# Attention products in 32-wide groups, and experts without a software pipeline

## The chip, the cores and the metric

The kernel runs on one core of a Trainium2 chip. Its time is device time in microseconds, from start to end of one execution. The core's engines run side by side, each with its own queue in strict order: TensorE (PE in the profile) multiplies matrices, with its weight loads shown apart as PEld; VectorE (DVE), ScalarE (ACT) and GpSimd (POOL) do elementwise work; SyncE (SP) issues the DMAs. Engines wait for each other by semaphores. TensorE multiplies a stationary operand of up to 128 rows (the contraction) by 128 columns (the outputs) with a moving operand and writes to PSUM, which has eight banks of 512 fp32 values in each of 128 partitions. All data here is fp32.

## The reference: a convolutional attention block, then attention and experts

The input is eight images of 256 channels by 32 x 32 pixels (1024 positions). Layer 0 normalizes each image, makes queries, keys (4 heads of 32) and values (4 heads of 64) by a 1x1 convolution, attends over all 1024 positions, adds a depthwise 3x3 convolution of the values, projects, and adds the result to the image:

```python
attn = jnp.einsum('bhkn,bhkm->bhnm', q, k) * SCALE
attn = jax.nn.softmax(attn, axis=-1)
out = jnp.einsum('bhdm,bhnm->bhdn', v, attn).reshape(B, Cc, H, W)
```

Then comes an FFN: a 1x1 convolution to 1024 channels, a depthwise 3x3 convolution, GELU of one half times the other, a 1x1 convolution back, and a filter in the Fourier domain of 8 x 8 patches. Layer 1 is causal attention over 1024 positions with 256 channels, followed by eight experts. Each expert is a chain of three matrices with a normalization and a ReLU after the first two; a weight per expert and position (`w`) mixes the outputs:

```python
h = jnp.einsum('bfd,edh->bfeh', x, W1) + b1
h = jax.nn.relu(_bn(h, g1, be1, m1, v1))
h = jnp.einsum('bfeh,ehk->bfek', h, W2) + b2
h = jax.nn.relu(_bn(h, g2, be2, m2, v2))
y = jnp.einsum('bfeh,ehd->bfed', h, Wo) + bo
return jnp.einsum('bfed,fe->bfd', y, w)
```

## The kernel before

The 256 channels lie in two groups of 128 partitions; positions run along the free dimension. `fast_body` does the work in three stages.

**Layer 0** goes image by image. `attend(b, c, fill)` (L381) takes half an image's queries, 512 of them, at a time. For each pair of heads `g` and each of eight key tiles `m` it makes a step: two logit products (L393), one per head, with the head's 32 rows of `qk` as the contraction, so that each sits on its own 32 rows of the array; one exponential on ScalarE for both (L395); and two value products (L397) that contract over the 128 keys. The stationary operand of the latter has 128 columns: 64 of values and 64 of ones, from a buffer `vT` that holds values, ones, values side by side. So one product gives a head's output and, in the other 64 rows, the sums for the softmax. There are 32 steps an image. The logits `s` have two buffers of two PSUM banks, the accumulators two banks, and all other products share two banks (`ps_m`, tag "mm"). After the eight key tiles ScalarE copies outputs and sums out (L404 to L407). `finish` (L409) divides by the sums: two reductions, a reciprocal, a product with `selh` that spreads the reciprocals over the channels (L418), then the projection.

After each step `attend` calls `fill` (L513). It draws pieces from generators that hold other work: `ffn` of the image before (`before`), `prologue` of the image after (`after`: norm, queries, keys, values, transposes of the values and the depthwise convolution), and `finish` of the half before (`late`). The share drawn grows with the number of the step, over STEPS = 32. A scheduler then orders instructions for each engine when the program is built, with these positions as priorities; at run time each engine works its list in order. The FFN's two depthwise convolutions a group are nine VectorE operations each (L462 and L464), from padded images `hpad` that ScalarE fills (L452). GELU (L472), the square root of the norms (L315) and the exponential make ScalarE change its function table, shown as ACT_TABLE_LOAD.

**Layer 1's attention** (L597) isn't touched by the change.

**The experts** (L754) run 128 units: 8 experts x 8 images x 2 halves of 512 positions. A unit has three layers of four products each (two output groups by two contraction groups): layer 1 (`pm<-z,w1s`), layer 2 (`pm<-h,w2s`), both at L724 with a ReLU on ScalarE (L728), and the output product (`pye`, L745), followed by a VectorE operation (L749) and an addition on GpSimd (L750). `advance(n)` (L731) is a software pipeline written by hand: it issues layer 1 of unit n, then layer 2 of unit n-1, then the output product of unit n-2. So between a layer and the next one of the same unit there are eight products of other units. All of them draw on one pool of eight PSUM banks.

Of the kernel before, what the change touches and what calls it, by code (L numbers as in the profile page):

```python
# [15 lines left out]
P = 128  # L16
# [62 lines left out]
def fast_body(  # L79
# [95 lines left out]
    with ExitStack() as l0:  # L175
# [3 lines left out]
        ps_s = l0.enter_context(tc.tile_pool(name="ps_s0", bufs=2, space=PSUM))  # L179
# [78 lines left out]
        def one_hot(dst, mult):  # L258
            nc.gpsimd.affine_select(
                out=dst,  # L260
                in_=dst,
                compare_op=ALU.not_equal,
                fill=1.0,
                base=0,
                pattern=[[-mult, dst.shape[1]], [0, dst.shape[2]]],
                channel_multiplier=1,
            )
# [3 lines left out]
        selh = rows_to("selh", 4, HD)  # L271
        one_hot(selh, 32)
# [9 lines left out]

        vts = []
        for i in range(2):
            v_ = one.tile([P, NT, KC, 3, HD], F32, tag=f"vT{i}", name=f"vT{i}")
            nc.gpsimd.memset(v_[:, :, :, 1, :], 1.0)
            vts.append(v_)

# [49 lines left out]
        def prologue(b):  # L338
# [5 lines left out]
            vT = vts[b % 2]  # L344
# [14 lines left out]
            for g in range(KC):  # L359
                for j0 in range(0, NT, 4):  # L360
                    tp = ps_m.tile([P, 4, 2, HD], F32, tag="mm", name="tpv")
                    for j in range(4):
                        nc.tensor.transpose(
                            tp[:, j].rearrange("p s d -> p (s d)"), o[:, g, (j0 + j) * P : (j0 + j + 1) * P], ident
                        )
                    nc.scalar.copy(vT[:, j0 : j0 + 4, g, 0:3:2, :], tp)
                yield
# [13 lines left out]
        def attend(b, c, fill):  # L381

            qk, vT, o = st[b]
            cs = slice(c * HALF, (c + 1) * HALF)
            sm = two.tile([P, HALF], F32, tag="sm", name="sm")
            ou = None
            for g in range(KC):
                acc = [ps_a.tile([P, HALF], F32, tag=f"acc{i}", name=f"acc{i}") for i in range(2)]
                for m in range(NT):
                    s = ps_s.tile([P, 2, HALF], F32, tag="s", name="s")  # L390
                    for i in range(2):
                        kp = slice((2 * g + i) * KD, (2 * g + i + 1) * KD)
                        nc.tensor.matmul(s[:, i, :], qk[kp, 1, m * P : (m + 1) * P], qk[kp, 0, cs], start=True, stop=True)  # L393
                    p = two.tile([P, 2, HALF], F32, tag="p", name="p", bufs=3)
                    nc.scalar.activation(p, s, AF.Exp)  # L395
                    for i in range(2):
                        nc.tensor.matmul(  # L397
                            acc[i], vT[:, m, g, i : i + 2, :], p[:, i, :], start=(m == 0), stop=(m == NT - 1)
                        )
                    fill()  # L400
                if g == 0:
                    ou = two.tile([P, KC, HALF], F32, tag="ou", name="ou", bufs=1)

                nc.scalar.copy(sm[64 * g : 64 * g + 32, :], acc[0][64:96, :])  # L404
                nc.scalar.copy(ou[0:64, g, :], acc[0][0:64, :])
                nc.scalar.copy(sm[64 * g + 32 : 64 * g + 64, :], acc[1][0:32, :])
                nc.scalar.copy(ou[64:128, g, :], acc[1][64:128, :])  # L407

            def finish():  # L409
# [6 lines left out]
                for g in range(KC):  # L416
                    bc = ps_m.tile([P, HALF], F32, tag="mm", name="bc")
                    nc.tensor.matmul(  # L418
                        bc, selh[:, 2 * g : 2 * g + 2, :], sm, start=True, stop=True
                    )  # L420
                    nc.vector.tensor_mul(ou[:, g, :], ou[:, g, :], bc)
                    nc.vector.tensor_add(o[:, g, cs], o[:, g, cs], ou[:, g, :])
                    nc.scalar.activation(t[:, g, cs], t[:, g, cs], AF.Identity, bias=proj_o[:, g : g + 1])
# [85 lines left out]
        STEPS = CH * KC * NT  # L509
        for b in range(B):  # L510
            step = [0]

            def fill():  # L513
                step[0] += 1
                i = step[0]
                if late is not None:
                    late.step()
                if i > 3 and before is not None:
                    before.to((i - 3) / (STEPS - 4))
                if after is not None:  # L520
                    after.to((i - 4) / (STEPS - 6))

# [174 lines left out]
    with ExitStack() as l2:  # L697
# [17 lines left out]


        units, hidden = [], {}

        def layer(name, w_, src, sc, bi, e):
            dst = hp.tile([P, KC, HALF], F32, tag=name, name=name, bufs=3)  # L720
            for g in range(KC):
                pm = ps.tile([P, HALF], F32, tag="mm", name="pm")
                for k in range(KC):
                    nc.tensor.matmul(  # L724
                        pm, w_[:, k, g * P : (g + 1) * P], src[:, k, :], start=(k == 0), stop=(k == KC - 1)
                    )
                c = KC * e + g
                nc.scalar.activation(dst[:, g, :], pm, AF.Relu, bias=bi[:, c : c + 1], scale=sc[:, c : c + 1])  # L728
            return dst

        def advance(n):  # L731
            if n <= len(units):
                e, b, h, w1s, w2s, wos, wb = units[n - 1]
                hidden[n - 1] = layer("h1", w1s, z[b][:, :, h * HALF : (h + 1) * HALF], s1, o1, e)
            if 0 <= n - 2 < len(units):
                e, b, h, w1s, w2s, wos, wb = units[n - 2]
                hidden[n - 2] = layer("h2", w2s, hidden[n - 2], s2, o2, e)
            if 0 <= n - 3:
                e, b, h, w1s, w2s, wos, wb = units[n - 3]
                h2 = hidden.pop(n - 3)  # L740
                hs = slice(h * HALF, (h + 1) * HALF)
                for g in range(KC):
                    py = ps.tile([P, HALF], F32, tag="mm", name="pye")
                    for k in range(KC):
                        nc.tensor.matmul(  # L745
                            py, wos[:, k, g * P : (g + 1) * P], h2[:, k, :], start=(k == 0), stop=(k == KC - 1)
                        )
                    y = hp.tile([P, HALF], F32, tag="y", name="y", bufs=3)
                    nc.vector.scalar_tensor_tensor(y, py, col("bo", KC * e + g), wb[:, hs], ALU.add, ALU.mult)  # L749
                    nc.gpsimd.tensor_add(t[b][:, g, hs], t[b][:, g, hs], y)  # L750
                if e == NE - 1 and h == 1:
                    nc.sync.dma_start(ov[b], t[b])

        for e in range(NE):  # L754
# [13 lines left out]
            for b in range(B):  # L768
                for h in range(2):
                    units.append((e, b, h, w1s, w2s, wos, wb))  # L770
                    advance(len(units))
        for i in range(2):
            advance(len(units) + 1 + i)
# [690 lines left out]
```

## Time and profile before

| | us |
|---|---|
| median of 3 runs | 3958.95 (3957.77 to 3959.01) |
| the profiled execution's own time | 3958.95 |
| its span in the trace | 3957.2 |
| TensorE busy | 3600.7 |
| VectorE busy | 1734.9 |
| ScalarE busy | 1349.2 |
| exponentials of layer 0 (L395), 256 of 1.022 | 255.0 |
| value and sum products (L397), 1024 records | 507.6 |
| logit products (L393), 1024 records | 316.2 |

A group line of the profile reads: line, engine, operation, output<-inputs, size of output<-input, count; then busy time in us and mean ns of one; then the engine's idle time before the group and what ended it. A matmul's size stands as rows*columns of the stationary operand, then the moving operand. Every fp32 product leaves two matmul records and two weight-load records. Records of TensorE overlap: the start of the next tells what one costs, and its length includes the drain. "PEclk" is the granted share of TensorE's clock.

### The profile page before, as it was taken

How to read it: one execution, taken by the hardware profiler on the slowest of the kernel's cores; microseconds unless marked ns; L12 is line 12 of the kernel's file. 1: busy time of each engine (PE TensorE's matmuls, PEld its weight loads, DVE VectorE, ACT ScalarE, POOL GpSimd, SP SyncE). 2: the span in 40 equal slices, each digit the busy share in tenths (PEclk: the TensorE clock that was granted, in tenths of full speed). 3: DMA queues.
4: the chain of work that ended last, by engine and by line, in shares of the span. 5: the costliest groups of instructions: out<-in, count | busy, mean ns of one | idle time of the engine just before them, and what ended most of it. 6: DMA issues, size and time to landing. Idle time of an engine off the chain costs nothing.

```text
span 3957.2 us, 25092 instructions
## 1 busy us (share of the span) xinstructions
PE 3600.7 (91%) x9780; PEld 1652.5 (42%) x9780; DVE 1734.9 (44%) x1946; ACT 1349.2 (34%) x1754; POOL 512.1 (13%) x483
## 2 busy tenths in 40 slices
PE   7999999999999998388878888889999999999998
PEld 4334343434343434244444444444444444444443
DVE  3377777676767685634444444321111111111111
ACT  4354545454545452021111112222333333333332
POOL 1000000000000000011112211122222222222222
PEclk9999999999999998688898889979999999999999
DMA  1000000000000000020000000000000000000001
GB/s 60 0 0 22 0 22 0 22 0 22 0 22 0 11 0 11 12 92 0 0 0 0 0 0 0 0 16 3 6 8 0 8 3 6 8 0 8 0 26 60
DMA packets 16277, 45.04 MB, mean 11 GB/s; under 512 B 1350, under 2 KB 9494, under 8 KB 14102
## 3 DMA queue, kind: packets, MB, share of 16 engines
q1 hardware_dynamic: 16150, 43.36, 3.0%
q8 instruction: 79, 1.29, 0.1%
q14 instruction: 48, 0.39, 0.0%
HBM read 26.57 MB, written 16.78 MB: 11 GB/s over the span
## 4 chain that ended last, share of the span: by engine, by line
PE 71%; DVE 19%; ACT 4%; issue 2%; POOL 2%; DMA 1%; ACTq 0%; SPq 0%; DVEq 0%; POOLq 0%
PE pm L724 22%; PE pye L745 11%; DVE conv L464 9%; PE acc L397 7%; PE s L393 3%; PE ph L330 3%; PE s L630 3%; PE po L661 3%; DVE o L377 3%; PE pq L607 3%; PE pz L480 3%; PE pq L330 2%; PE var L574 2%; DVE r L577 1%; PE pv L617 1%
## 5 line engine op out<-in xcount | busy, mean ns | idle before, releaser
L728 ACT ACTIVATE h<-pm,bn_o,bn_s 128x512 f32<-128x512 f32 x512 | 398.5, 778 | 894.1 <-PE pm L724 894.1
L749 DVE SCALAR_TENSOR_TENSOR y<-pye,vec,wb 128x512 f32<-128x512 f32 x256 | 192.1, 750 | 1148.0 <-PE pye L745 1148.0
L464 DVE SCALAR_TENSOR_TENSOR conv<-hpad,vec,conv 128x1024 f32<-128x1024 f32 x512 | 648.5, 1279 | 9.4
L397 PE MATMUL acc<-p,vT 128*128 128x512 f32 x1024 | 507.6, 628 | 62.3 <-ACT p L395 61.9
L724 PE MATMUL pm<-z,w1s 128*128 128x512 f32 x1024 | 463.0, 595 | 0.0
L724 PE MATMUL pm<-h,w2s 128*128 128x512 f32 x1024 | 460.3, 592 | 0.0
L745 PE MATMUL pye<-h,wos 128*128 128x512 f32 x1024 | 460.2, 592 | 0.0
L750 POOL TENSOR_TENSOR t<-t,y 128x512 f32<-128x512 f32 x256 | 324.3, 1267 | 1031.3 <-DVE y L749 1031.3
L397 PEld LDWEIGHTS acc<-p,vT 128*128 128x128 f32 x1024 | 192.2, 197 | 338.8 <-issue 173.0
L395 ACT ACTIVATE p<-s 128x1024 f32<-128x1024 f32 x256 | 255.0, 1022 | 218.0 <-PE s L393 217.1
L393 PE MATMUL s<-qk 32*128 32x512 f32 x1024 | 316.2, 632 | 0.0
L724 PEld LDWEIGHTS pm<-z,w1s 128*128 128x128 f32 x1024 | 194.7, 191 | 249.1 <-issue 192.4
L724 PEld LDWEIGHTS pm<-h,w2s 128*128 128x128 f32 x1024 | 194.6, 190 | 244.9 <-issue 213.6
L745 PEld LDWEIGHTS pye<-h,wos 128*128 128x128 f32 x1024 | 194.6, 190 | 244.9 <-issue 244.9
L330 PE MATMUL ph<-xn,piw 128*128 128x512 f32 x512 | 246.1, 613 | 18.1 <-ACT hpad L452 18.1
L630 PE MATMUL s<-kk,q 128*128 128x512 f32 x512 | 236.4, 597 | 10.4 <-DVE pr L648 5.6
L574 PE MATMUL var<-sq,mean_c 128*128 128x512 f32 x128 | 107.6, 946 | 123.8 <-POOL sq L571 123.8
L558 POOL MEMSET ones<- 1x128 f32 x1 | 0.2, 194 | 1633.3 <-DVE conv L464 1633.3
L393 PEld LDWEIGHTS s<-qk 32*128 32x128 f32 x1024 | 93.0, 184 | 180.3 <-issue 165.5
L377 DVE SCALAR_TENSOR_TENSOR o<-vpad,pe_w,o 128x1024 f32<-128x1024 f32 x128 | 161.8, 1275 | 0.3
L330 PEld LDWEIGHTS ph<-xn,piw 128*128 128x128 f32 x512 | 95.4, 194 | 157.3 <-issue 127.4
L480 PE MATMUL pz<-pow__122,hid 128*128 128x256 f32 x512 | 121.9, 389 | 42.8 <-DVE hid L473 42.8
(177 smaller groups left out, 3239.0 us busy)
## 6 DMA issues: line engine op xcount, KB each, us to landing
t<-in_x_dram SPq DMA_DIRECT2D x8, 1024.0 KB, 4.9
sp<-t SPq DMA_DIRECT2D x8, 1024.0 KB, 3.9
t<-sp SPq DMA_DIRECT2D x8, 1024.0 KB, 9.9
out_dram<-t SPq DMA_DIRECT2D x8, 1024.0 KB, 4.0
w1s<-in_w_dram SPq DMA_DIRECT2D x8, 256.0 KB, 2.7
w2s<-in_w_dram SPq DMA_DIRECT2D x8, 256.0 KB, 2.8
wos<-in_wo_dram SPq DMA_DIRECT2D x8, 256.0 KB, 2.7
piw<-in_pi_wT_dram SPq DMA_DIRECT2D x1, 1024.0 KB, 8.7
```

Source lines behind the costliest of these rows:

```text
L330: nc.tensor.matmul(ps, w[:, k, o0 : o0 + P], src[:, k, hs], start=(k == 0), stop=(k == KC - 1))
L377: nc.vector.scalar_tensor_tensor(d3, src, wk, d3, ALU.mult, ALU.add)
L393: nc.tensor.matmul(s[:, i, :], qk[kp, 1, m * P : (m + 1) * P], qk[kp, 0, cs], start=True, stop=True)
L395: nc.scalar.activation(p, s, AF.Exp)
L397: nc.tensor.matmul(acc[i], vT[:, m, g, i : i + 2, :], p[:, i, :], start=(m == 0), stop=(m == NT - 1))
L464: nc.vector.scalar_tensor_tensor(d3, src, wk, d3, ALU.mult, ALU.add)
L480: nc.tensor.matmul(pz[:, k, :], hid[g][:, (2 * n + k) * P : (2 * n + k + 1) * P], pow_[:, g, :], start=(g == 0), stop=(g == ng - 1),)
L630: nc.tensor.matmul(s[:, hs], q[:, k, q0 : q0 + P], kk[:, k, hs], start=(k == 0), stop=(k == KC - 1))
L724: nc.tensor.matmul(pm, w_[:, k, g * P : (g + 1) * P], src[:, k, :], start=(k == 0), stop=(k == KC - 1))
L728: nc.scalar.activation(dst[:, g, :], pm, AF.Relu, bias=bi[:, c : c + 1], scale=sc[:, c : c + 1])
L745: nc.tensor.matmul(py, wos[:, k, g * P : (g + 1) * P], h2[:, k, :], start=(k == 0), stop=(k == KC - 1))
L750: nc.gpsimd.tensor_add(t[b][:, g, hs], t[b][:, g, hs], y)
```

## The change

Two edits. In layer 0 the attention steps are cut differently: a step now covers all four heads, two key tiles and 256 queries. There are four logit products per key tile, each on its own 32 rows of the array (L395 of the new kernel), and two exponentials of 128 x 1024. The values are taken in pieces of 32 channels, so that each product writes 32 output partitions on its own 32 columns of the array, with four pieces for each pair of heads (L406). The sums are products of their own, with a stationary operand of 32 columns, 16 of them ones (L413). The ones between the values are gone. There are 16 steps an image instead of 32, the logits have one buffer of four banks instead of two of two, the accumulators and sums take one bank each, and the shares in `fill` are set anew. In the experts, the pipeline is taken out: each unit does layer 1, layer 2 and the output product in turn (L754 and L769 of the new kernel).

```diff
-        ps_s = l0.enter_context(tc.tile_pool(name="ps_s0", bufs=2, space=PSUM))
+        ps_s = l0.enter_context(tc.tile_pool(name="ps_s0", bufs=1, space=PSUM))
...
+        ones32 = wpool.tile([P, 2, 32], F32, name="ones32")
+        nc.gpsimd.memset(ones32, 0.0)
+        for c in range(2):
+            nc.gpsimd.memset(ones32[:, c, 16 * c : 16 * c + 16], 1.0)
...
-            for g in range(KC):
-                acc = [ps_a.tile([P, HALF], F32, tag=f"acc{i}", name=f"acc{i}") for i in range(2)]
-                for m in range(NT):
-                    s = ps_s.tile([P, 2, HALF], F32, tag="s", name="s")
+            for part in range(2):
+                ps_ = slice(c * HALF + part * QC, c * HALF + (part + 1) * QC)
+                acc = ps_a.tile([P, KC, QC], F32, tag="acc", name="acc")
+                for m2 in range(NT // 2):
+                    s = ps_s.tile([P, NH, 2, QC], F32, tag="s", name="s")
                     for i in range(2):
-                        kp = slice((2 * g + i) * KD, (2 * g + i + 1) * KD)
-                        nc.tensor.matmul(s[:, i, :], qk[kp, 1, m * P : (m + 1) * P], qk[kp, 0, cs], start=True, stop=True)
-                    p = two.tile([P, 2, HALF], F32, tag="p", name="p", bufs=3)
-                    nc.scalar.activation(p, s, AF.Exp)
+                        m = 2 * m2 + i
+                        for hd in range(NH):
+                            kp = slice(hd * KD, (hd + 1) * KD)
+                            nc.tensor.matmul(
+                                s[:, hd, i, :], qk[kp, 1, m * P : (m + 1) * P], qk[kp, 0, ps_], start=True, stop=True
+                            )
+                    p = two.tile([P, NH, 2, QC], F32, tag="p", name="p")
+                    for g in range(KC):
+                        nc.scalar.activation(p[:, 2 * g : 2 * g + 2], s[:, 2 * g : 2 * g + 2], AF.Exp)
                     for i in range(2):
-                        nc.tensor.matmul(
-                            acc[i], vT[:, m, g, i : i + 2, :], p[:, i, :], start=(m == 0), stop=(m == NT - 1)
-                        )
+                        m = 2 * m2 + i
+                        for g in range(KC):
+                            for q in range(4):
+                                nc.tensor.matmul(
+                                    acc[32 * q : 32 * q + 32, g, :],
+                                    vT[:, m, g * P + 32 * q : g * P + 32 * q + 32],
+                                    p[:, 2 * g + q // 2, i, :],
+                                    start=(m == 0 and g == 0), stop=(m == NT - 1), skip_group_check=True,
+                                )
+                        for hd in range(NH):
+                            nc.tensor.matmul(
+                                sums[32 * hd : 32 * hd + 32, :], ones32[:, part, :], p[:, hd, i, :],
+                                start=(part == 0 and m == 0), stop=(part == 1 and m == NT - 1),
+                            )
                     fill()
...
-        STEPS = CH * KC * NT
+        STEPS = CH * NT
...
-                    before.to((i - 3) / (STEPS - 4))
+                    before.to((i - 3) / (STEPS - 3.5))
                 if after is not None:
-                    after.to((i - 4) / (STEPS - 6))
+                    after.to((i - 2) / (STEPS - 3))
...
-        units, hidden = [], {}
...
-                    units.append((e, b, h, w1s, w2s, wos, wb))
-                    advance(len(units))
-        for i in range(2):
-            advance(len(units) + 1 + i)
+                    hs = slice(h * HALF, (h + 1) * HALF)
...
+                    h1 = hp.tile([P, KC, HALF], F32, tag="h1", name="h1")
+                    layer(h1, w1s, z[b][:, :, hs], s1, o1)
+                    h2 = hp.tile([P, KC, HALF], F32, tag="h2", name="h2")
+                    layer(h2, w2s, h1, s2, o2)
+                    for g in range(KC):
+                        py = ps.tile([P, HALF], F32, tag="mm", name="pye")
...
```

The `layer` function keeps its body (two output groups, each with two products and a ReLU) and takes its destination as an argument; `h1` and `h2` have two buffers instead of three. `finish` works on 256 columns of sums with two `selh` tables, one per part, and two products of 256 columns where one of 512 stood. The evacuation is one copy of 128 x 512 per part and one of 128 x 256 for the sums per half image.

## The prediction

> **What bounds the kernel now.** I read the page first: the shares of the engines, the forty slices and the chain that ended last.
>
> ```profile
> span 3957.2 us, 25092 instructions
> PE 3600.7 (91%) x9780; PEld 1652.5 (42%) x9780; DVE 1734.9 (44%) x1946; ACT 1349.2 (34%) x1754; POOL 512.1 (13%) x483
> PE   7999999999999998388878888889999999999998
> DVE  3377777676767685634444444321111111111111
> PE 71%; DVE 19%; ACT 4%; issue 2%; POOL 2%; DMA 1%; ACTq 0%; SPq 0%; DVEq 0%; POOLq 0%
> ```
>
> TensorE bounds both places that the change touches: slices 1 to 15 (layer 0) and the last 13 (experts). In layer 0 VectorE is second at 7 tenths, so there is room below TensorE, but it ends. I then cut the span at the second reciprocal of each image (L414), which gives layer 0's periods: 125 us for image 0, 184, 195, 194, 194, 198, 195 and 185 for the others, then a tail to 1676. Busy time in such stretches:
>
> ```profile
> core 0: us, PE busy (x) PEld busy (x) DVE busy (x) ACT busy (x) POOL busy (x), PEclk, DMA share, GB/s
> 565.00:759.00 194.00, 183.62 (x544) 79.24 (x544) 141.42 (x134) 97.80 (x118) 0.00 (x0) 0.98 0.03 11
> 1531.00:1685.00 154.00, 72.85 (x204) 37.93 (x204) 106.13 (x103) 22.59 (x33) 0.19 (x1) 0.73 0.05 17
> 2640.00:3957.00 1317.00, 1306.98 (x3041) 575.88 (x3039) 192.18 (x261) 396.77 (x514) 321.77 (x254) 1.00 0.03 10
> ```
>
> A steady image leaves TensorE idle only 10.4 us of 194. The tail is VectorE's. The experts leave it 10 us idle in 1317.
>
> Next, what one product costs, from the timeline of layer 0 (start, length, engine, line):
>
> ```profile
> 784.58 0.64 PE L310 MATMUL ms<-xn,mean_c 128*32 128x256 f32 x8
> ...
> 808.21 1.88 PE L397 MATMUL acc<-p,vT 128*128 128x512 f32 x4
> 810.02 1.13 PE L393 MATMUL s<-qk 32*128 32x512 f32 x4
> 811.08 1.98 PE L330 MATMUL ph<-xn,piw 128*128 128x512 f32 x4
> 812.90 1.90 PE L397 MATMUL acc<-p,vT 128*128 128x512 f32 x4
> ```
>
> One source product leaves two records. Full-array records of 512 columns start 0.429 us apart, so a product takes 0.858. The four `s` records are two heads on two row groups: from 810.02 to 811.08 is 1.06 us, where two products in series would take 1.72. So row groups run together. The `ms` line is eight records, four products of 256 columns on four column groups, in 0.64 us with the drain; in series they would need 4 x 0.43 = 1.72. So column groups run four wide. Changing the array's shape costs: `acc` to `s` is 1.81 for 1.716 of streaming, `s` 1.06 for 0.858, `ph` 1.82 for 1.716. That is 0.39 for two changes, so 0.2 us per entry into rows or the full array; I take 0.12 into columns, since weights of 32 columns load in 0.11 against 0.19.
>
> The experts' handover, from their timeline:
>
> ```profile
> 3002.23 3.60 PE L724 MATMUL pm<-h,w2s 128*128 128x512 f32 x8
> ...
> 3004.15 0.78 ACT L728 ACTIVATE h<-pm,bn_o,bn_s 128x512 f32<-128x512 f32 x1 [0.94 <-PE pm L724]
> 3005.66 3.60 PE L745 MATMUL pye<-h,wos 128*128 128x512 f32 x8
> 3005.87 0.78 ACT L728 ACTIVATE h<-pm,bn_o,bn_s 128x512 f32<-128x512 f32 x1 [0.94 <-PE pm L724]
> ```
>
> The last of eight records starts at 3005.23, and ScalarE starts 0.63 later. TensorE meanwhile works on another unit. And how ScalarE releases TensorE, with what the exponentials cost in a steady image (565 to 759):
>
> ```profile
> 948.16 0.59 ACT L488 COPY zf<-pz 128x512 f32<-128x512 f32 x1 [3.46 <-PE pz L480]
> 948.80 0.30 PEld L490 LDWEIGHTS pf<-zf,dft 128*128 128x128 f32 x2 [0.65 <-ACT zf L488]
> ```
>
> ```profile
> L397 PE MATMUL acc<-p,vT 128*128 128x512 f32 x128 | 63.6, 629 | 8.6 <-ACT p L395 8.5
> L395 ACT ACTIVATE p<-s 128x1024 f32<-128x1024 f32 x32 | 32.0, 1022 | 21.4 <-PE s L393 21.2
> L395 ACT ACT_TABLE_LOAD x8 | 10.3, 1283 | 4.0 <-PE s L393 3.9
> ```
>
> ScalarE ends at 948.75 and the weight load starts 0.05 later. Of the 10.4 us idle, 8.5 are waits for exponentials.
>
> **What the Trainium skill says.** "TensorE: Matmul & The Clock Gate", Part 3: products in different row or column groups run concurrently; four rows measured 3.07x. The trace agrees for two rows and four columns; four rows are not shown. "TensorEngine Tiling (Array Packing)", Key Properties: a change of tiling mode drains the array; here that is the 0.2 us. "ScalarE: Activation LUTs", Table sets: exponential, square root and GELU anchor different sets, so alternating them reloads; here 1283 ns each, eight times an image before an exponential. The first page, Part 2, gives TensorE a queue of 64; no row here shows its depth.
>
> **The experts, part by part.** Both kernels run 128 units of 12 products. Without the pipeline, layer 2 follows layer 1 of the same unit at once, and the output product follows layer 2. Weights, ScalarE, VectorE and GpSimd work and DMAs stay. Let the last record of a layer start at T. Its stream ends at T+0.43; the next layer's first product needs only the first half of `h`, long done, and runs to T+1.29. The second product needs the other half: T + 0.63 + 0.78 + 0.05 = T+1.46. So 0.17 us of wait, plus 0.10 because its weights can't load ahead of the wait (a first record alone spans 0.53 instead of 0.43, as after an array change). That is 0.28 per handover, two per unit, 256 in all: **+71 us**. Behind it queue only later products; the eight banks, VectorE and GpSimd have slack. Ends: +55 if the weight load is partly hidden, +95 if ScalarE starts 0.1 later.
>
> **Attention, TensorE.** Per image before: 32 pairs of logits (27.5 us) and 64 value products (54.9), 82.4 together. After: 128 logits in fours of two 0.215 us records (32 x 0.43 = 13.8), 256 value products in 64 fours (27.5), and 128 products for the sums in 32 fours (13.8): 55.0. Saved: 27.4. In the built order some groups are split by filler: about ten pairs before (4.3 us), five fours after (2.1). Array entries in a steady image: before 30 into rows, 29 into full, 2 into columns, 12.0 us; after 22, 35 and 21, 13.9. Everything else (FFN, projections, norms) is unchanged, 84 us. Stream sums: 178.3 before, 150.8 after, **-27.5**. Check: 178.3 / 0.98 clock + 10.4 idle = 192, observed 194.
>
> **Attention, waits.** The logits now fill four banks, once instead of twice, so a step is serial: logits, two exponentials, products, next logits. From the last logit record to the first value product: 0.63 + 1.02 + 0.05 = 1.7, and 0.4 more until the second exponential is through, about 2.1 us of cover needed, where one exponential needed 1.3. In the built order the filler there is, step by step, 0.9, 1.3, 1.7, 1.7, 8.6, 2.6, 1.7, 1.7, 2.6, 1.3, 1.7, 3.4, 2.6, 1.3, 0 and 2.1 us: 7 us short over the image. Eight steps have a table load too, bound to the exponential and so behind the logits, some with a GELU queued ahead that itself waits for VectorE's convolution. 1.28 each, little of it covered: 8 x 1.28 = 10. I take 18 us where 8.5 stood: +9.5. Ends: 8.5 again (the filler covers) and 32 (24 more).
>
> **Attention, the rest.** Evacuation shrinks from 128 copies of 0.58 to 48, on ScalarE, which isn't the bound. VectorE loses 4 us an image (reciprocals over 256 columns, 1.75 against 3.35, and smaller reductions): 137 in a period near 175, second still. The one-off memsets change by a few, under the first loads. Layer 1 is untouched.
>
> **Sum.** Images 2 to 6: 27.5 - 9.5 = 18 each, 90. Image 1: stream 160.2 to 127.7, less 9.5: 23. Image 7: 177.1 to 140.8, less 9: 27. Image 0 has little filler (17.5 us short, with the first prologue outside), stream down 32, added waits about 14: 18. Two FFN bands slip into VectorE's tail: -4. Layer 0: **-154**. The execution's own time is 3958.95, its span 3957.2 and 1.75 around it; it equals the median of the three. 3958.95 - 154 + 71 = **3876 us**.
>
> **Rivals.** A, the filler covers the exponentials as well as now (8.5 us an image): for, the scheduler placed it there; against, only one logit buffer. Layer 0 gains 154 + 7.5 x 9.5 = 225: 3805 us. B, slower: ScalarE's strict order holds up the exponential (table load, GELU waiting for VectorE), and with one buffer each delay stops TensorE. The gain per image must stay above 71 / 7.5 = 9.5, so it decides when the added wait passes 18 us an image, 1.1 us a step. With 24 it is 7.5 x 3.5 = 26 gained, 3958.95 - 26 + 71 = 4004 us. For: waits up to 3.9 us on exponentials stand already; against: they sum to only 8.5. C, the groups don't run four wide or TensorE can't be fed: a step now issues 128 records and loads. If logits ran as pairs, 13.8 more an image, 3876 + 110 = 3986. Feeding: ms starts come 7 ns apart but in a burst; a sustained rate below 56 ns per instruction isn't shown. D, the experts' stalls vanish in the queue: 3805.
>
> **How the numbers follow.** My forecast 0.65, A 0.12, B 0.12, C 0.05, D 0.04, and 0.02 for a half-way B near 3958. The likeliest's own range is 3835 to 3925 (waits 12 to 26 an image, experts 60 to 85). The 8-in-10 range takes in A and D and stops short of B and C: 3800 to 3950. A measurement can tell about 0.2% from no change. So faster is 0.65 + 0.12 + 0.04 = 0.81, same 0.02, slower 0.12 + 0.05 = 0.17.
>
> **What would show it.** Right: image periods near 175; `s` records four abreast, `acc` groups starting 0.215 apart in fours; idle before `acc` for `p` near 18 us an image; in the experts a 0.2 to 0.3 us gap before the third record of each L754 and L769 group on `h`, the stage 71 longer. Wrong: `s` or `acc` starting in series, periods above 185, VectorE as releaser in layer 0's chain, or no gaps in the experts.

## The result and the profile after

The changed kernel takes 4015.16 us (median of four, 4008.28 to 4017.69) against 3958.36 for the kernel before (four, 3955.81 to 3959.01). The ratio is 1.0142, with a 95% interval of 1.0124 to 1.016: 57 us slower, where 83 us faster was forecast.

From the page of the changed kernel: span, busy time of the engines, VectorE in forty slices, and the chain that ended last.

```profile
span 4015.8 us, 37305 instructions
PE 3507.8 (87%) x15988; PEld 1675.8 (42%) x15988; DVE 1694.4 (42%) x1946; ACT 1284.2 (32%) x1672; POOL 509.9 (13%) x486
...
DVE  3385858584858587444444444311111111111111
...
PE 66%; DVE 23%; ACT 5%; issue 3%; POOL 2%; DMA 1%; SPq 0%; ACTq 0%; POOLq 0%; DVEq 0%
```

TensorE works 93 us less (3600.7 to 3507.8), and the span is 58.6 longer, so 151.5 us of idle time are new. VectorE's row has changed its look: where layer 0 showed sevens and sixes it now swings between 4 or 5 and 8, once an image. Its share of the chain rose from 19% to 23%; VectorE as a releaser in layer 0 was on the list of what would show the forecast wrong, and so were image periods above 185.

Two landmarks split the 58.6. The first product of layer 1 (`mu`) starts at 1673.0 where it started at 1685.4, and the first of the experts (`pm<-z`) at 2598.8 instead of 2611.4. So layer 0 gained 12.5 us of the forecast 154, layer 1 is unchanged, and the experts last 1417.0 instead of 1345.8: 71.2 longer, where 71 was forecast. Cut at the second reciprocal of each image, layer 0 reads:

| | before | after | difference | forecast |
|---|---|---|---|---|
| image 0 | 185.6 | 175.1 | -10.5 | -18 |
| image 1 | 184.0 | 182.8 | -1.2 | -23 |
| images 2 to 6, mean | 195.3 | 198.0 | +2.7 (five: +13) | -18 (five: -90) |
| image 7 | 184.9 | 171.5 | -13.4 | -27 |
| tail to `mu` | 154.1 | 153.8 | -0.3 | +4 |

A steady image has become longer. Waits of TensorE over images 2 to 6 (us in all, times, longest), first the kernel before, then the changed one:

```profile
PE acc L397 <- ACT p L395: 40.5, 50, 3.1
```

```profile
PE acc L406 <- ACT p L400: 51.5, 29, 6.9
PE pz L497 <- DVE hid L490: 46.6, 10, 6.4
PE rb L322 <- DVE r L316: 27.8, 10, 3.4
PE pp L330 <- DVE o L439: 23.6, 10, 2.5
```

The waits for exponentials grew by 11 us over five images, 2.2 an image. The other three are new or nearly so (`pz` had 2.9 us before, the other two nothing): `pz` is the FFN's last convolution waiting for the product with GELU, `rb` the norm's broadcast waiting for its reciprocal, `pp` the projection waiting for the division. They are 98 us, 19.6 an image, and VectorE ends each.

Why VectorE, at 137 us in an image of 198? Cut one image into slices of 24 us (the columns are length, then PE, PEld, DVE, ACT and POOL busy with counts, clock, DMA share, GB/s). Before:

```profile
855.20:879.20 24.00, 22.49 (x68) 8.99 (x67) 23.75 (x24) 12.19 (x18) 0.00 (x0) 1.00 0.00 1
879.20:903.20 24.00, 23.28 (x61) 8.77 (x60) 24.00 (x23) 13.48 (x15) 0.00 (x0) 1.00 0.00 0
903.20:927.20 24.00, 21.63 (x62) 8.55 (x60) 24.00 (x23) 11.22 (x15) 0.00 (x0) 1.00 0.00 1
```

After, two early and three late slices of an image:

```profile
750.70:774.70 24.00, 23.65 (x200) 15.15 (x203) 7.39 (x12) 5.05 (x6) 0.00 (x0) 1.00 0.24 85
774.70:798.70 24.00, 17.78 (x188) 8.59 (x180) 7.69 (x8) 16.84 (x19) 0.00 (x0) 0.93 0.01 4
...
846.70:870.70 24.00, 20.77 (x188) 11.55 (x180) 23.89 (x24) 14.18 (x19) 0.00 (x0) 1.00 0.00 1
870.70:894.70 24.00, 20.42 (x129) 8.40 (x132) 23.12 (x24) 8.37 (x10) 0.00 (x0) 0.86 0.00 1
894.70:918.70 24.00, 15.17 (x170) 8.18 (x162) 24.00 (x23) 11.35 (x14) 0.00 (x0) 0.96 0.00 1
```

VectorE is a third busy early in the image and without a pause later. It was full late in the image before the change too, for the same three slices or 72 us; there TensorE had almost enough work to cover it, 67.4 us. After, it has 56.4. Once attention costs TensorE less, that stretch lasts as long as VectorE's work, and TensorE stands. The two halves of an image tell the same: from one second reciprocal to the next first one it went from 107.9 to 100.0 us, and from there to the second from 86.4 to 97.7 (images at 759.2 and 750.7).

Not every wait that VectorE ends comes from its load. The two for `rb` fall early in this image, from 785.8 and 797.5 on, where VectorE has time:

```profile
787.42 1.75 DVE L316 RECIPROCAL r<-r 128x256 f32<-128x256 f32 x1 [2.91 <-ACT r L315]
789.23 2.47 PE L322 MATMUL rb<-r,sel 128*128 128x256 f32 x8 [3.43 <-DVE r L316]
```

VectorE itself stood idle for 2.91 us here. The norm's chain (table load and square root on ScalarE, reciprocal on VectorE) runs in series, and the next product in TensorE's list is the one that waits for its end.

The order of the queues does the rest. In the timeline of the changed kernel (start, length, engine, line; in brackets the idle time before and what ended it):

```profile
911.78 1.15 PE L395 MATMUL s<-qk 32*128 32x256 f32 x16
916.82 0.63 ACT L489 ACTIVATE hid<-conv 128x512 f32<-128x512 f32 x1 [9.17 <-DVE conv L481]
917.47 1.28 ACT L400 ACT_TABLE_LOAD   x1
918.76 1.94 ACT L400 ACTIVATE p<-s 128x1024 f32<-128x1024 f32 x2
919.84 2.00 PE L406 MATMUL acc<-p,vT 128*32 128x256 f32 x16 [6.91 <-ACT p L400]
```

The logits are done near 913. ScalarE has a GELU ahead of the exponential; GELU waits 9.17 us for VectorE's convolution; then come a table load and the exponential. TensorE's wait is booked on ScalarE, and its root is for the larger part VectorE: of the 6.91 us, 3.9 pass until GELU can start, and 1.9 with GELU and the table load.

The long gaps cost a second time. Granted clock (the third column from the end) behind a gap of 3.06 us that ends at 908.40, and behind the one of 6.91 us:

```profile
908.40:910.40 2.00, 2.00 (x30) 1.23 (x34) 2.00 (x3) 0.00 (x0) 0.00 (x0) 1.00 0.00 0
919.84:921.84 2.00, 2.00 (x20) 0.79 (x24) 2.00 (x3) 1.98 (x2) 0.00 (x0) 0.50 0.04 8
```

In this image there are five stretches of 3.4 to 6.8 us with a lowered clock, and they cost 10.5 us of products. Over images 2 to 6 the mean is 11.1 an image, against 5.0 before (busy time at the lowered clock, times the share of the clock that was missing). "TensorE: Matmul & The Clock Gate" of the Trainium skill, Part 1, says that an idle window of about 3.4 us halves the rate and about as much sustained work restores it; the gap of 6.91 us agrees: then 0.50, and 1.00 again from 923.84 on. But shorter gaps are followed by a lowered clock as well. In the kernel before, a gap of 3.06 us from 731.55 on, as long as the one without a loss here, is followed by

```profile
734.70:738.10 3.40, 3.40 (x4) 1.05 (x4) 3.37 (x4) 3.36 (x4) 0.00 (x0) 0.50 0.00 0
```

and one of 2.00 us (from 801.02 on) by 3.3 us at 0.50. So the length of a single gap doesn't decide it, and what does isn't shown here.

So a steady image adds up, with the forecast's stream sums: the stream, -27.5; idle time 9.7 to 31.8, +22.1; busy time above the stream sum (185.6 less 178.3 before, 166.2 less 150.8 after), +8.1, of which the clock accounts for 6.1. The sum is +2.7, as observed; it must be, since a period is busy time plus idle time, and what it shows is the sizes of the parts.

In the experts, timeline of the changed kernel:

```profile
2999.46 3.88 PE L754 MATMUL pm<-h,w2s 128*128 128x512 f32 x8
3006.89 3.60 PE L754 MATMUL pm<-z,w1s 128*128 128x512 f32 x8
```

The group that reads `h` of its own unit is 0.28 longer than the one that doesn't. Inside it, the start of the record that waits comes 0.604 us after the one before it, 0.175 more than the stream's 0.429, and the next start 0.533 later, 0.104 more, since its weights could not load ahead.

### The profile page after: what moved, and what is told of

The parts are those of the page before. It is cut to its first block, busy times and chain, and to the rows that moved or that the text cites. A ratio compares the mean times of both kernels' runs of the same rounds, so it can differ in the third digit from the quotient of the medians.

```text
span 4015.8 us, 37305 instructions
## 1 busy us (share of the span) xinstructions
PE 3507.8 (87%) x15988; PEld 1675.8 (42%) x15988; DVE 1694.4 (42%) x1946; ACT 1284.2 (32%) x1672; POOL 509.9 (13%) x486
## 4 chain that ended last, share of the span: by engine, by line
PE 66%; DVE 23%; ACT 5%; issue 3%; POOL 2%; DMA 1%; SPq 0%; ACTq 0%; POOLq 0%; DVEq 0%
PE pm L754 23%; PE pye L769 12%; DVE conv L481 11%; PE acc L406 3%; PE pz L497 3%; DVE o L375 3%; PE s L647 3%; PE po L678 3%; PE pq L624 3%; PE ph L330 3%; PE pq L330 2%; PE var L591 2%; PE sums L413 2%; DVE r L594 1%; PE pv L634 1%
## 5 line engine op out<-in xcount | busy, mean ns | idle before, releaser
L754 PE MATMUL pm<-h,w2s 128*128 128x512 f32 x1024 | 494.5, 605 | 1.4
L769 PE MATMUL pye<-h,wos 128*128 128x512 f32 x1024 | 494.5, 605 | 1.4
L754 PE MATMUL pm<-z,w1s 128*128 128x512 f32 x1024 | 463.3, 595 | 0.0
L406 PE MATMUL acc<-p,vT 128*32 128x256 f32 x4096 | 344.1, 419 | 85.2 <-ACT p L400 85.2
L754 PEld LDWEIGHTS pm<-h,w2s 128*128 128x128 f32 x1024 | 184.0, 189 | 291.1 <-issue 153.3
L769 PEld LDWEIGHTS pye<-h,wos 128*128 128x128 f32 x1024 | 184.0, 189 | 291.0 <-issue 183.7
L754 PEld LDWEIGHTS pm<-z,w1s 128*128 128x128 f32 x1024 | 194.7, 191 | 249.2 <-issue 195.9
L406 PEld LDWEIGHTS acc<-p,vT 128*32 128x32 f32 x4096 | 140.0, 117 | 262.7 <-ACT p L400 161.3
L413 PE MATMUL sums<-p,ones 128*32 128x256 f32 x2048 | 235.0, 403 | 0.0
L497 PE MATMUL pz<-pow__122,hid 128*128 128x256 f32 x512 | 136.3, 420 | 95.0 <-DVE hid L490 95.0
L395 PE MATMUL s<-qk 32*128 32x256 f32 x2048 | 172.6, 403 | 0.0
L469 ACT ACTIVATE hpad<-ph,pi_o 128x512 f32<-128x512 f32 x128 | 87.4, 689 | 252.7 <-PE ph L330 249.2
```

What stands on the lines that cost most here:

```text
L406: nc.tensor.matmul(acc[32 * q : 32 * q + 32, g, :], vT[:, m, g * P + 32 * q : g * P + 32 * q + 32], p[:, 2 * g + q // 2, i, :], start=(m = ...
L413: nc.tensor.matmul(sums[32 * hd : 32 * hd + 32, :], ones32[:, part, :], p[:, hd, i, :], start=(part == 0 and m == 0), stop=(part == 1 and ...
L497: nc.tensor.matmul(pz[:, k, :], hid[g][:, (2 * n + k) * P : (2 * n + k + 1) * P], pow_[:, g, :], start=(g == 0), stop=(g == ng - 1),)
L754: nc.tensor.matmul(pm, w_[:, k, g * P : (g + 1) * P], src[:, k, :], start=(k == 0), stop=(k == KC - 1))
L769: nc.tensor.matmul(py, wos[:, k, g * P : (g + 1) * P], h2[:, k, :], start=(k == 0), stop=(k == KC - 1))
```

## The experiments

Two theories are set against each other for layer 0. V: VectorE sets the time, since its work comes due in the second half of an image and TensorE waits for it, directly or through GELU. E: the exponential path sets it (one logit buffer, ScalarE's order, table loads), which is rival B of the prediction. In an experiment's name "attn" is the new attention with the pipelined experts, and "before" the old attention. The kernels with 6 and 3 taps leave out three and six of the nine taps of the FFN's depthwise convolution; the one with ReLU computes ReLU in place of GELU.

### Each half of the change alone

The first kernel has the new attention and the experts of before; the second the reverse.

> The attention part of the change alone; the experts keep their pipeline. Measured so far: whole change +57 us, and the experts' gaps in its trace are 0.278 us at each of 256 handovers, 71 us. Theory V (VectorE's work in layer 0 comes in two phases, nearly idle in the first third of an image and saturated after it, so an image still takes about 197 us although TensorE has 27 us less to stream) and rival E (each exponential, with one buffer of logits and table loads in its way, stops TensorE) both expect 3958 - 13 = 3945 us, within 5. If the two parts disturb each other, it lies off that.

> The experts' part alone, in the kernel before. 256 handovers of 0.278 us: 3958 + 71 = 4029 us, within 4. A rival that takes the handover for hidden by TensorE's queue: 3958.

Measured: 3942.52 us, ratio 0.9954 (0.9937 to 0.997), 19 us faster than before on the same chip; and 4034.19 us, ratio 1.0183 (1.0162 to 1.0203), 73 slower. -19 and +73 give +54, against the +57 of both together. The experts' term stands, and the whole error lies in layer 0, whose images are as long as in the changed kernel (198.0 in the steady ones).

### Less VectorE work, six taps

```diff
-                    for k in range(9):
+                    for k in range(6):
...
-                        if k % 3 == 2:
+                        if k % 2 == 1:
```

The same edit in the new and in the old attention. It removes about 31 us of VectorE work an image and none of TensorE's.

> The attention part alone, with three of the nine taps of the FFN's depthwise convolution left out (so 8 x 3 x 1.28 = 31 us of VectorE work less an image; TensorE, ScalarE and DMAs unchanged). Theory V: images 1 to 6 shrink by 25 to 30 us each and the tail by 30, so about 200 us below the attention part alone. Rival E (exponentials): only the tail, 30 us, and some waits on the hidden units, 60 us below in all.

> The kernel before with the same three taps left out. It is bound by TensorE's stream, 182 us of 194 an image, so it can gain the tail (30 us) and at most the 10 us of waits an image: 40 to 100 us. If it gains as much as the attention part does (about 200), VectorE sets both and theory V explains nothing particular to the change.

Measured: 3796.0 (0.9585, 0.9566 to 0.9604), a steady image of 179.5; and 3907.34 (0.9866, 0.9847 to 0.9886), a steady image of 191.8. The new attention gains 146 us from VectorE work taken away, the old one 54; the tail after the last image is 25 and 30 of that. V is right in kind: work that costs TensorE nothing sets the pace in the new kernel. It gives back 18.5 us an image of the 31 removed, less than V's figure (25 to 30), so VectorE's load isn't the whole bound. E alone, with 60 us in all, falls far short.

### No change of tables

```diff
-                    nc.scalar.activation(blocks[:, k], halves[0][:, k].rearrange("p (n r) c -> p n r c", r=PS), AF.Gelu)
+                    nc.scalar.activation(blocks[:, k], halves[0][:, k].rearrange("p (n r) c -> p n r c", r=PS), AF.Relu)
```

> The attention part alone, with the FFN's GELU computed as a ReLU (so the GELU itself and the table loads around it, 12 to 14 of 1.28 us an image on ScalarE, are left out). In the attention part alone TensorE waits 87 us in layer 0 for exponentials. Rival E (the exponential's wait with its table loads is what ate the gain): 50 to 85 us faster than the attention part alone. Theory V (VectorE saturated in the later two thirds, so an earlier exponential only makes TensorE wait elsewhere): 0 to 25 faster.

Measured: 3892.5, ratio 0.9837 (0.9817 to 0.9857), 50 us less than the new attention with GELU; a steady image takes 188.4. Each taken against the kernel before on its own chip (3956.98 and 3961.42), the difference is 46. So it lies at the lower edge of the range given for E, 50 to 85, and above V's, 0 to 25. Over layer 0 the waits for exponentials fell from 86.7 to 55.6, and `pz` from 94.9 to 72.7. So the table loads (16 an image with GELU, 4 without) matter as well, 9.6 us an image: they lie on the way of VectorE's results through ScalarE as much as on the exponentials' own. V alone falls with this run, as E alone fell with the taps; parts of both stand.

### VectorE's work earlier

Three edits change when VectorE's work is issued, and leave nothing out. "Early" starts the FFN of the image before at step 2 and draws the late projection twice as fast. "Moved" takes the values' depthwise convolution out of the end of the image before and puts it into the first four steps of its own image, where VectorE is a third busy; the rest of the prologue is then drawn from step 3 on, in fewer pieces. The last has both, with the FFN from step 3.

```diff
                     late.step()
-                if i > 3 and before is not None:
-                    before.to((i - 3) / (STEPS - 3.5))
+                    late.step()
+                if i > 1 and before is not None:
+                    before.to((i - 1) / (STEPS - 1.5))
```

```diff
-        PRO_PIECES = 2 + 4 + 2 + 6
+        PRO_PIECES = 2 + 4 + 2
...
+        CONV_PIECES = 6
+        def value_conv(b):
...
+                conv.to(i / CONV_STEPS)
...
-                if after is not None:
-                    after.to((i - 2) / (STEPS - 3))
+                if i > 2 and after is not None:
+                    after.to(max(2 / PRO_PIECES, (i - 2) / (STEPS - 3)))
...
+            conv = Stream(value_conv(b), CONV_PIECES)
```

> The attention part alone, with the FFN of the image before started in step 2 instead of 4 and the last half's projection drawn two pieces a step instead of one. Each step is now about 12 us, so the start after the third step, kept from the 32-step schedule, holds VectorE's work back twice as long as before. Theory V: VectorE's idle third shrinks by up to two steps, 8 to 20 us an image, 50 to 130 us in all. Rival E: within 20.

> The attention part alone, with the depthwise convolution of the values (22 us of VectorE an image) taken out of the prologue, late in the image before, and drawn in the first four steps of its own image, where VectorE idles. Nothing is left out. The run with three taps less took 18 us off an image for 31 us of VectorE. Theory V: 22 us moved out of the saturated stretch shorten an image by 13 to 22 us, 90 to 150 us in all, 3795 to 3855. Rival E: within 25 of the attention part alone.

> Both of these: values' convolution in the first steps of its own image, FFN drawn from step 3, last projection two pieces a step. Theory V: VectorE's work spread evenly leaves TensorE's stream of 154 us and its waits, an image near 165 to 175, so 3740 to 3810 us. Rival E: within 40 of the attention part alone.

Measured: 3921.97 (0.9912, 0.9892 to 0.9931), 3895.66 (0.9843, 0.9826 to 0.9859) and 3884.88 (0.982, 0.9803 to 0.9836): 20, 47 and 58 us less than 3942.52, with steady images of 191.7, 191.7 and 189.0. Each falls short of V's figures, and the second and third go beyond E's; the first is at the edge of E's (within 20). In the last kernel the waits for exponentials have grown to 137.6 us over layer 0, 97 of them with a GELU just ahead. Most of the direct waits on VectorE went, and the wait moved to the queue behind GELU.

### GELU one convolution later

GELU and its product are issued one group later, after the first half of the next group, so that its input has been ready longer; `conv` gets a third buffer. The second kernel has the edits of the last one above too. Theory Q, in what was expected, joins V and E: a VectorE that is behind in the late stretch stops TensorE directly and through ScalarE's strict order.

```diff
+                    if side == 1 and late_gate is not None:
+                        late_gate()
...
-                    dst = two.tile([P, N], F32, tag="conv", name="conv")
+                    dst = two.tile([P, N], F32, tag="conv", name="conv", bufs=3)
...
+                def gate(halves=halves):
...
+                late_gate = gate
+            late_gate()
```

> The attention part alone, with each group's GELU (and its product) issued one convolution later, so that it stands behind work already done; a third buffer for the convolutions allows it. Nothing is left out. In the attention part alone 52 of the 87 us that TensorE waits for exponentials fall where ScalarE reaches a GELU that still waits for VectorE's convolution, with the exponential queued behind it. Theory Q (a VectorE behind in the later two thirds stops TensorE through ScalarE's order and through TensorE's own order): 25 to 55 us faster than the attention part alone, 3887 to 3917. Theory V alone (VectorE's total and its idle start, whatever the order): within 10.

> The values' convolution in its own image's first steps, the FFN drawn from step 3, and the GELU one convolution later, together. With the first two alone TensorE waited 97 us behind a GELU and 138 for exponentials in all. Theory Q: 40 to 90 us less than those two alone, 3795 to 3845. Theory V alone: within 10 of those two, about 3885.

Measured: 3918.19 (0.9907, 0.9891 to 0.9924), 24 less than the new attention alone, and 3880.8 (0.981, 0.9794 to 0.9827), only 4 less than without the gate. The first is just short of Q's range (25 to 55 less) and more than the 10 of V alone. The second misses Q's, but it doesn't test it: GELU still stands where it stood on ScalarE, since the scheduler put it there again (over the image from 709.0 on, ScalarE's 102 instructions have the same order with and without the edit). Waits of TensorE in it from 332 to 1266 us, which is five steady images:

```profile
PE acc L412 <- ACT p L406: 91.9, 35, 7.0
```

That is 18.4 us an image. The kernel is the fastest version that computes everything, 76 us below the kernel before on the same chip (3956.41), with the experts' pipeline kept.

### The experts, half the handovers

The attention is the old one; in layer 2 the contraction index runs outside, over two banks, so that each half of `h` is used for both output groups before the next is needed.

```diff
-                    layer(h2, w2s, h1, s2, o2)
+                    pm = [ps.tile([P, HALF], F32, tag="mm", name="pm") for g in range(KC)]
+                    for k in range(KC):
+                        for g in range(KC):
+                            nc.tensor.matmul(
+                                pm[g], w2s[:, k, g * P : (g + 1) * P], h1[:, k, :], start=(k == 0), stop=(k == KC - 1)
+                            )
+                    for g in range(KC):
...
+                            h2[:, g, :], pm[g], AF.Relu, bias=o2[:, c : c + 1], scale=s2[:, c : c + 1]
```

> The experts' part alone, with the four products of layer 2 in the order of the contraction half first, output group second, so that the second half of h is needed one product (0.86 us) later. If the 0.278 us is the wait for that half and nothing else, the handover from layer 1 to layer 2 costs nothing; the one to the output product stays, since its first half comes out one product later and the first product waits instead. So half of the loss: about 3958 + 36 = 3994. If a handover costs what it costs whatever the order (a drain, say): 4029 to 4034, unchanged.

Measured: 3993.93, ratio 1.0097 (1.008 to 1.0113), 37.5 slower than before, where the kernel with both handovers is 73 slower. One handover of two is gone and half the loss with it: the experts last 1381.2 us, against 1345.8 with the pipeline and 1416.8 with both handovers. So the loss is those waits, and nothing else about the missing pipeline shows.

### Three taps

The six-tap edit with three taps, in both attentions, to see whether the forecast's period appears when VectorE has room.

> The attention part alone, with six of the nine taps of the FFN's depthwise convolution left out: 61 us less of VectorE an image. The forecast put an image at 175 with VectorE free. Theory Q (waits for VectorE, direct and through ScalarE, and the clock lost in them, ate the gain): image 165 to 173, 18 to 25 less than the kernel before with the same taps left out; about 3690 to 3730 us. If the 32-wide products or their array changes themselves cost more than their stream, the image stays at 178 or more as with three taps less, and the time above 3745.

> The kernel before with the same six taps left out. Bound by TensorE's stream: image 188 to 192 (191.8 with three taps less), the tail 30 us shorter; 3850 to 3885 us.

Measured: 3731.46 (0.9428, 0.9408 to 0.9448), a steady image of 175.2; and 3857.62 (0.9747, 0.9726 to 0.9768), 189.3. The forecast's period was 175, and here it is, though slightly above the 165 to 173 expected of this run, and only 14.1 below the old attention's, where 18 to 25 were expected. That the number is the forecast's is luck in part: the forecast had 18 us of waits for exponentials in it and none on VectorE. What the new attention is worth against the old one, with the same taps in both, is 19 us with nine taps, 111 with six and 126 with three, of the 154 forecast for layer 0. Waits of TensorE with three taps, 334 to 1162:

```profile
PE rb L322 <- DVE r L316: 27.9, 10, 3.4
PE pp L330 <- DVE o L439: 17.1, 10, 1.9
PE acc L406 <- ACT p L400: 10.3, 8, 1.8
```

The exponentials, the subject of the forecast's wait term, hardly count here: 10.3 us in all, about 2 an image. With one logit buffer and two exponentials the filler covers a step, as long as nothing holds ScalarE up. Table loads alone don't: 12 an image still stand there. `rb` and `pp` stay, since there VectorE's own chains (square root, reciprocal; sums, division) come one after the other with TensorE.

### The values' convolution on GpSimd

GpSimd is idle in layer 0, so the values' convolution (nine taps of 128 x 1024 a group) was moved to it, first alone and then with the earlier shares.

```diff
-                        nc.vector.scalar_tensor_tensor(d3, src, wk, d3, ALU.mult, ALU.add)
+                        nc.gpsimd.tensor_scalar(tap3, src, wk, 1.0, ALU.mult, ALU.mult)
+                        nc.gpsimd.tensor_add(d3, d3, tap3)
```

> The attention part alone, with the values' depthwise convolution on GpSimd, which has nothing to do in layer 0: nine multiplications and eight additions per channel group instead of nine fused operations, so 22 us less of VectorE and some 85 us of GpSimd an image. Nothing is left out. Theory Q: 13 to 22 us an image, 90 to 140 us in all, 3800 to 3850. If GpSimd slows VectorE down by as much, or the projection then waits for it: 3900 or more.

> The same with the FFN drawn from step 3 and the last projection two pieces a step (20 us by themselves). Theory Q: 20 to 50 us below the version on GpSimd alone, 3760 to 3830.

Measured: 4104.18 (1.0368, 1.0349 to 1.0386) and 4075.31 (1.0302, 1.0283 to 1.032), steady images of 223.1 and 216.4. Both miss Q's ranges; the first is in the other case expected, 3900 or more. Groups of the first from 560 to 760 us (mean ns of one behind the busy time), and its largest wait for VectorE from 350 to 1346:

```profile
L378 POOL TENSOR_TENSOR o<-o,tap 128x1024 f32<-128x1024 f32 x12 | 38.0, 3164 | 0.9
L484 DVE SCALAR_TENSOR_TENSOR conv<-hpad,vec,conv 128x1024 f32<-128x1024 f32 x60 | 104.4, 1744 | 1.9
```

```profile
PE pp L330 <- DVE o L442: 117.9, 8, 21.6
```

VectorE's operation takes 1744 ns on average instead of 1279. Over layer 0, the 140 of these operations that fall almost wholly beside GpSimd's work take 2494 ns, and the 296 that don't meet it 1284. And `o`, which needs GpSimd's result, is late by up to 21.6 us. Relief for VectorE by another engine was no relief here; as a test of V by the load alone, the run is inconclusive.

## Why the prediction was wrong

**The experts** were right: 0.278 a handover forecast and measured, +71 and 71.2, and the sub-terms too (0.17 of wait, 0.10 of weight load).

**TensorE's streams** were right. `s` goes four abreast, sixteen records in 1.15 us; groups of `acc` start 0.215 apart in fours, sixteen in 1.06. With the clock's losses taken off, an image's busy time went from 180.6 (185.6 less 5.0) to 155.1 (166.2 less 11.1), 25.5 less where 27.5 was forecast. The terms as listed in the working add up to 182.7 and 155.0 and not to 178.3 and 150.8; their difference, 27.7, is hardly touched by that. Rival C (not four wide, or not fed) is out.

**The waits for exponentials** were put too high: +2.2 us an image measured, +9.5 taken. And what grew has another root than the one costed. Over layer 0 with the new attention alone they are 86.7 us, in which ScalarE spends 32.0 with exponentials, 15.0 with table loads, 6.3 with GELU, and 26.5 idle before a GELU that waits for VectorE's convolution; the rest is small. Before it was 61.9, with 41.9, 13.9, 1.3 and 0.1. So the growth is about as large as the wait for VectorE, and the table loads hardly grew.

**The failed step** is "137 in a period near 175, second still", which set TensorE's waits on VectorE at nothing. The total was right (136.9) and the test was the wrong one. A sum over an image says nothing of when the work is due: the values' convolution, the FFN's and the division all come in its second half, where VectorE had been full for 24 us slices on end before the change. In the changed kernel direct waits on VectorE of 19.6 us an image arose, against 1.2 before (the FFN's and a transpose's). About half of them are VectorE's load: `pz`, 9.3 us, is gone from the steady images with three taps left out. `rb` and `pp`, 10.3 us together, hang on the order: 9.0 us of them remain with six taps left out, while with the same work issued earlier (the last kernel of "VectorE's work earlier") `rb` falls to 0.6 and `pp` is gone, and a new wait of 2.6 for the sums' reciprocal comes in. The forecast priced neither. Its bound was an average over stages with different limits, though slices of 24 us of the kernel before show the full stretch.

**The clock** was left out of the change: 178.3 / 0.98 was used as a check of before, and the lowered clock behind the new gaps, 6.1 us an image more than before, wasn't carried into after.

**The smaller images** missed as well: image 1 gained 1.2 of 23, image 7 13.4 of 27. Image 0, with no FFN beside it, gained 10.5 of 18. Their waits weren't traced apart.

**The rivals.** B's end (4004) is near the time, and its condition, more than 18 us of added wait an image, was met with 22. Its mechanism is right only in part: it placed the waits on the exponential behind ScalarE's order, and those grew by 2.2; the ReLU run shows that the table loads do cost some 50 us in all, about half of it through results of VectorE that pass ScalarE. A's premise, exponentials covered as well as before, is nearer the measured waits (10.3 an image against 8.1) than the forecast's own term, but its time (3805) is far off, since VectorE took the gain. D is out.

**What is open.** How much of the loss is VectorE's load in the late phase, and how much is the order of GELU on ScalarE, isn't fully separated: taps (146 us for three of nine), table loads (50) and places (58) overlap. The best version's remaining wait (18.4 us an image for exponentials) sits behind GELU. A kernel that holds GELU back by a true dependency wasn't tried, nor one that gives `rb` and `pp` other work to wait behind and changes nothing else.

## What to carry to other kernels

When one engine is relieved, test the next one in each stretch where it is already full, and not over a whole period: there the period can shrink only as far as that engine's own work allows. In the three slices of before, TensorE had 67.4 us of work and VectorE 71.75 of 72, so with VectorE's work where it was hardly anything could be gained in them. Look also for short chains over several engines that the relieved engine has no other work to cover. New gaps in TensorE were paid twice here, since its clock fell behind them. And a serial handover is priced well by the record starts of the old kernel: wait for the producer, plus the weight load that can't run ahead.

## What the runs showed of the hardware

- GpSimd's and VectorE's elementwise work slow each other: VectorE's `scalar_tensor_tensor` of 128 x 1024 fp32 took 2494 ns beside GpSimd's work and 1284 without it, and GpSimd's addition of the same size 3132 ns with VectorE busy and 2352 with VectorE idle (layer 0 of the kernel with the values' convolution on GpSimd).
- Four row groups with 32 rows each, and four column groups with 32 outputs each, run abreast at 256 columns: groups of four start 0.215 us apart, with four records and four weight loads in each, 27 ns an instruction.
- Behind a gap of 6.91 us TensorE's clock was halved for about 4 us of work. Of two gaps of 3.06 us one was followed by half the clock for 3.4 us and one by none, and a gap of 2.00 by half the clock for 3.3.
- A product that waited for a semaphore paid 0.104 us more in the experts: its weight load starts with it (3000.494 and 3000.496), not ahead of it.
